# A graph layer on one core: 126 rows instead of 128 per gather, 51 fillers instead of 53, and the first list of single rows ahead of the block numbers

## The chip, the cores and the metric

One core of one Trainium2 chip runs the whole program. The metric is the device time of one execution in microseconds (us). The kernel before takes 15128.52 us, the median of three runs (15126.48 to 15129.18). One more execution was profiled: it took 15126.4 us, of which the span from its first to its last instruction is 15124.7 us.

## The reference

The input is a graph of N = 50,000 nodes with 128 fp32 features each, and E = 1,650,000 edges (`src`, `dst`, a type of 0 or 1), sorted by `dst`. Each node has one edge to itself (a loop), so 50,000 of the edges have `src == dst`. Cut to what matters:

```python
Xs = X[src]                                   # one row of 512 bytes per edge
msg = jnp.where((edge_types == 0)[:, None], Xs @ W_data.T + b_data, Xs @ W_control.T + b_control)
agg = jax.ops.segment_sum(msg, dst, num_segments=N)
y = jax.nn.relu(agg + X @ W_self.T + b_self)
out = _layernorm(X + y, axis=-1)
```

Since the message is linear in the row, the kernel first sums the rows of `x` per destination node and type, and multiplies by the weights once per node.

## The kernel before, in words

**Blocks and steps.** The sorted list of edges is cut into NBLK = 431 blocks. A block is worked on in Q = 2 steps, and a step of an ordinary block takes 1917 edges, whose rows of `x` reach SBUF in three ways:

- R = 14 gathers of 128 rows each (`SIZES = [P] * R`, 1792 edges). A gather is one indirect DMA on GpSimd (POOL) with a list of row numbers, line 551 in `gathers`.
- S = 72 single rows, each a DMA of 512 bytes with its address in a register: the list of step 0 is issued by SyncE (SP), that of step 1 by ScalarE (ACT), line 585 in `single_rows`. Ahead of each 24 of them the queue loads 24 addresses into registers (line 580).
- F = 53 fillers. An edge that is a loop needs no gathered row, as the row of `x` is there anyway. So each loop among the 1792 edges leaves a hole, and the kernel puts the edge of a filler in its place. `fill` (lines 388 to 417) does it on VectorE (DVE) with arrays of 30 x 63 numbers per partition (63 = F + LATE, LATE = 10 being the fillers that may be handed on to the next step); a loop's own row comes in by `left_out_columns` to `left_out_rows`.

Block 0 and the last block are plain: they have gathers alone. The last block takes what is left, 1640 edges in 13 gathers: twelve of 128 rows and one of 104.

**What a block does then.** DVE compares each edge's column with the numbers 0 to 127 (`onehot`, line 507: which of 64 nodes, which type) and counts per column (line 515). TensorE (PE) multiplies the gathered rows by the one-hot matrices (line 607; line 613 for the 72 single rows) into PSUM, DVE adds that to the block's sums (line 621), PE applies the weights (lines 641 to 651), DVE and ACT do the layer norm, and SP stores 124 nodes.

**What sets the order.** The instructions stand on each engine in the order in which the program writes them. What matters around the change:

- POOL does nothing but gathers after its first few microseconds. `y`, into which a step's 14 gathers go, has five buffers, so POOL may be up to five steps ahead of PE.
- `pace` (lines 533 to 542) holds POOL back against the lists of single rows: from block FAR = 4 on, the k-th gather of block b waits until SP and ACT have both issued the lists of all blocks up to b, and k of 28 parts of the lists of block b + 1. SP and ACT count that up as they issue.
- The lists are issued up to FAR = 4 blocks ahead, into ten buffers (five for each queue), which PE gives back after line 613.
- At the start, `columns(0)` computes the first ten blocks' columns and the byte addresses of the single rows (line 191) on DVE. `block_numbers` (lines 236 to 248) computes, also on DVE but some 25 us later, where each block's nodes begin, and `window(0)` lets SP load these numbers into registers (line 483) and fetch a stretch of the transposed `x` (line 490). Ahead of the loop over the blocks stand, in this order: `columns(0)`, `spread(1)`, `fill(1)`, `block_numbers()`, `window(0)`, work on the blocks 0 to 2, and the lists `single_rows(1)` to `single_rows(3)`.

If some step had more than LATE fillers waiting to be handed on, a flag would be set at the end, and a second, general version of the layer would run after this one (`general`). In the profile it doesn't run.

Of the kernel before, what the change touches and what calls it, by code (L numbers as in the profile page):

```python
# [26 lines left out]
P = 128  # L27
# [6 lines left out]
R = 14  # L34
# [2 lines left out]
PASS = 7  # L37
B = 124
C = R * Q
F = 53  # L40
LATE = 10
FX = LATE + F
R1 = R + 1
H = R + 1
C1 = Q * R1
SIZES = [P] * R
SIZE = sum(SIZES)
CE = Q * SIZE
S = 72
LOAD = 24  # L50
BE = CE + Q * (F + S)
NBLK = 2 + (E + LATE - CE) // BE
REST = E + LATE - CE - (NBLK - 2) * BE
REST_ROWS = [min(n, max(0, REST - q * SIZE - sum(SIZES[:r]))) for q in range(Q) for r, n in enumerate(SIZES)]
RCH = sum(n > 0 for n in REST_ROWS)
assert len(SIZES) == R and sum(REST_ROWS) == REST
GB = 10
# [4 lines left out]
FAR = 4  # L62
# [29 lines left out]
def plain(b):  # L92

    return b == 0 or b >= NBLK - 1
# [6 lines left out]
def straight(ctx, tc, c, x, x_t, edges_t, edges_f, edges_1, dst_first, first_p, out):  # L101
# [70 lines left out]
    fills_f = keep.tile([P, 1], F32, name="fills_f")  # L172
    nc.vector.memset(fills_f, float(F))
    last_f = keep.tile([P, 1], F32, name="last_f")
# [112 lines left out]
    def columns(g):  # L287
        for _ in column_steps(g):
            pass

    def column_steps(g):
# [82 lines left out]
        stay = eds.tile([P, GB, C1], F32, name="stay")  # L374
        nc.vector.scalar_tensor_tensor(stay, rk, F - LOOP, v, op0=ALU.is_ge, op1=ALU.mult)
        col_g[g], rk_g[g], stay_g[g], cb_g[g], vp_g[g] = col, rk, stay, cb, v_f
# [3 lines left out]
    def spread(b):  # L380

        if plain(b):
            return
        g, i = divmod(b, GB)
        vf = lists[b % 2][:, :Q * FX]
        nc.tensor.matmul(vf, row_of[:, i:i + 1].to_broadcast([STACK, P]), vp_g[g], start=True, stop=True)

    def fill(b):

        if plain(b):  # L390
            return
        g, i = divmod(b, GB)
        two = lists[b % 2]
        vf, cb = two[:, :Q * FX], two[:, Q * FX:]
        nc.vector.tensor_copy(cb, cb_g[g][:, i, :])  # L395
        m = fil.tile([P, C1, FX], F32, name="m", bufs=1)
        nc.vector.tensor_tensor(m, rk_g[g][:, i, :, None].to_broadcast([P, C1, FX]),  # L397
                                rank_no_ps[:, None, :].to_broadcast([P, C1, FX]), op=ALU.is_equal)
        new = fil.tile([P, C1, FX], F32, name="new", bufs=1)
        nc.vector.tensor_tensor(new.rearrange("p (q r) f -> p q r f", r=R1), m.rearrange("p (q r) f -> p q r f", r=R1),  # L400
                                vf.rearrange("p (q f) -> p q f", f=FX)[:, :, None, :].to_broadcast([P, Q, R1, FX]),
                                op=ALU.mult)
        v = fil.tile([P, C1], F32, name="v_new")
        nc.vector.tensor_reduce(v, new, AX.X, ALU.add)  # L404
        vi = fil.tile([P, C1], I32, name="vi")
        nc.vector.tensor_tensor(vi, v, stay_g[g][:, i, :], op=ALU.add)
        idx = fil.tile([P, C1], I32, name="idx", bufs=RAHEAD + 2)
        nc.vector.tensor_single_scalar(idx, vi, COLS.bit_length() - 1, op=ALU.logical_shift_right)
        nc.vector.scalar_tensor_tensor(col_g[g][:, i, :], idx, -float(COLS), vi, op0=ALU.mult, op1=ALU.add)
        idxs[b] = idx  # L410

        old = fil.tile([P, C1, FX], F32, name="new", bufs=1)
        nc.vector.tensor_tensor(old, m, cb[:, :, None].to_broadcast([P, C1, FX]), op=ALU.mult)  # L413
        by = fil.tile([P, Q, FX], BF16, name="by")
        with nc.allow_low_precision(reason="whole numbers below 256, one of them not 0"):
            nc.vector.tensor_reduce(by, old.rearrange("p (q r) f -> p q f r", r=R1), AX.X, ALU.add)  # L416
        bys[b] = by
# [37 lines left out]
    def column(k):  # L455
        return k // R * R1 + k % R
# [54 lines left out]
    def counts(b):  # L511

        cnt = ohp.tile([P, Q, 2 * W], BF16, name="cnt")
        with nc.allow_low_precision(reason="whole numbers up to R1"):
            nc.vector.tensor_reduce(cnt, ohs[b].rearrange("p (q r) w -> p q w r", r=R1), AX.X, ALU.add)  # L515
        cnts[b] = cnt
# [12 lines left out]
    def mark(q):  # L529
        (nc.scalar if q else nc.sync).sem_inc(issued[q], 1)  # L530
        issued_no[q] += 1

    def pace(b, k):

        if b < FAR:
            return
        for q in range(Q):
            if (b + LAG, q) in marks:
                n = marks[b + LAG, q] + k
                if n > asked[q]:  # L540
                    nc.gpsimd.wait_ge(issued[q], n)
                    asked[q] = n

    def gathers(b, ks):
# [3 lines left out]
        for k in ks:  # L548
            pace(b, k)
            r = REST_ROWS[k] if b == NBLK - 1 else SIZES[k % R]  # L550
            copy = nc.gpsimd.indirect_dma_start(  # L551
# [16 lines left out]
    def single_rows(b):  # L568
        if plain(b):
            return  # L570
        g, i = divmod(b, GB)
        for q in range(Q):
            j = alone_no[0] % ALONE
            alone_no[0] += 1
            marks[b, q] = issued_no[q]
            y = one.tile([S, D], F32, name="y1")
            for s0 in range(0, S, LOAD):
                n = min(LOAD, S - s0)
                at = i * Q + q
                _, regs = nc.values_load_multi_w_load_instructions(  # L580
                    off_g[g][at:at + 1, s0:s0 + n], engines=[ACT if q else SP], min_val=0, max_val=(N - 1) * ROW,
                    skip_runtime_bounds_check_because=CLAMPED)
                for k, r in enumerate(regs):
                    r = nc.s_assert_within(r, 0, (N - 1) * ROW, skip_runtime_bounds_check_because=CLAMPED)
                    copy = (nc.scalar if q else nc.sync).dma_start(y[s0 + k:s0 + k + 1, :].bitcast(U8),  # L585
                                               x_bytes[bass.ds(r, ROW)].rearrange("(p e) -> p e", e=ROW))
                    copy.then_inc(alone[j], 16)
                    tc.no_tile_sem_insts.add(copy.ins.name)
                    tc.add_to_no_dep_group(f"single{b}_{q}", copy.ins)
                    while issued_no[q] - marks[b, q] < (s0 + k + 1) * C // S:  # L590
                        mark(q)
            got[j] += 16 * S
            singles[b, q] = y, alone[j], got[j]

    def products(b, q, ks):
# [9 lines left out]
        for k in ks:  # L605
            r = REST_ROWS[k] if b == NBLK - 1 else SIZES[k % R]
            nc.tensor.matmul(acc[:, :2, :].rearrange("p t w -> p (t w)"), y[:r, k % R, :], ohs[b][:r, column(k), :],  # L607
# [116 lines left out]
        nc.vector.tensor_copy(c["bad"], total)  # L724

    columns(0)
    spread(1)
    fill(1)
    block_numbers()
# [9 lines left out]
    for b in range(1, AHEAD):  # L739
        onehot(b)  # L740
        counts(b)
    for b in range(1, FAR):
        single_rows(b)
    made, fresh = 2, [2]
    ready = []
# [72 lines left out]
    b = NBLK - 1  # L818
# [230 lines left out]
def gnn_resnorm(  # L1049
# [46 lines left out]
    with ExitStack() as own:  # L1096
        straight(own, tc, c, x, x_t, edges_t, edges_f, edges_1, dst_first, first_p, out)
# [61 lines left out]
```

## Time and profile before

| | |
|---|---|
| median of three runs | 15128.52 us |
| profiled execution | 15126.4 us |
| its span | 15124.7 us |
| first gather starts / last gather ends | 3.33 us / 15109.26 us |
| gathers | 12,053 |
| busy share of POOL, DVE, PE, PE's weight loads, ACT | 75%, 80%, 38%, 36%, 0% |
| mean busy share of the 16 DMA engines | 20.1% for the gathers, 3.1% for the rest |

The instructions that issue a DMA on SP and ACT aren't counted as busy time, so ACT's 0% says nothing of how full its queue is. A POOL record of a gather ends when the gather has been handed to the DMA engines, not when its rows have landed. DVE has the highest share of busy time, but a share is an average: what counts is which engine never waits.

### The profile page before, as it was taken

What the parts mean: (1) busy time and instruction counts of PE and PEld (TensorE: products, weight loads), DVE (VectorE), ACT (ScalarE), POOL (GpSimd) and SP (SyncE); (2) the same over time, 40 slices, a digit from 0 to 9 for tenths busy, and PEclk for the clock granted to TensorE, in tenths of its full rate; (3) what the DMA queues carried; (4) which work ended last, traced back from release to release, by engine and by line L of the source; (5) the groups of instructions that cost most, each with busy time, mean ns of one, the idle gap of its engine ahead of it and who ended that gap; (6) DMA issues with size and microseconds to landing.
All of it is one profiled execution on the core that took longest, in us unless ns stands there. A gap on an engine that the chain in (4) does not pass through costs nothing.

```text
span 15124.7 us, 261323 instructions
## 1 busy us (share of the span) xinstructions
PE 5807.3 (38%) x32944; PEld 5433.6 (36%) x32945; DVE 12113.2 (80%) x12021; ACT 67.2 (0%) x222; POOL 11400.6 (75%) x12063
## 2 busy tenths in 40 slices
PE   3434333333333333333333333333333333333333
PEld 3333333333333333333333333333333333333333
DVE  9888888878787787888887778787888888778785
ACT  0000000000000000000000000000000000000000
POOL 6777777777777777777777777777777777777777
PEclk7666666666666666666666666666666666666666
DMA  2222222222222222222222222222222222222222
GB/s 60 61 62 60 61 60 60 61 60 61 61 60 60 61 60 60 61 60 60 61 60 60 63 60 62 60 60 62 60 60 62 60 60 61 61 60 61 60 60 57
DMA packets 583259, 916.02 MB, mean 61 GB/s; under 512 B 259900, under 2 KB 375957, under 8 KB 581474
## 3 DMA queue, kind: packets, MB, share of 16 engines
q0 software_dynamic: 385696, 790.66, 20.1%
q1 hardware_dynamic: 133564, 92.41, 2.2%
q10 hardware_dynamic: 62214, 16.14, 0.5%
q14 instruction: 1518, 12.44, 0.3%
q8 instruction: 267, 4.37, 0.1%
HBM read 870.81 MB, written 27.36 MB: 59 GB/s over the span
## 4 chain that ended last, share of the span: by engine, by line
ACTq 29%; SPq 21%; PE 19%; issue 16%; DMA 10%; POOL 3%; DVE 2%; PEldq 0%; PEld 0%; POOLq 0%; ACT 0%; DVEq 0%
ACTq L585 24%; PE acc L607 18%; SPq L585 17%; DMA y<-in_x,idx 10%; ACTq L580 5%; SPq L580 3%; POOL y L551 3%; PE acc L613 1%; ACTq L530 1%; SPq L530 0%; PE rank L320 0%; DVE cnt L515 0%; DVE by L416 0%; PE acc L616 0%; PEldq L558 0%
## 5 line engine op out<-in xcount | busy, mean ns | idle before, releaser
L551 POOL DMA_INDIRECT y<-in_x,idx x12040 | 11386.8, 946 | 3703.5 <-issue 1808.4
L607 PE MATMUL acc<-oh,y 128*128 128x128 f32 x24106 | 4731.8, 381 | 9047.4 <-PEq L558 8980.3
L607 PEld LDWEIGHTS acc<-oh,y 128*128 128x128 f32 x24106 | 4529.5, 290 | 9357.9 <-issue 5094.8
L515 DVE TENSOR_REDUCE cnt<-oh 128x256 bf16<-128x3840 f32 x431 | 2840.3, 6590 | 14.7
L507 DVE TENSOR_TENSOR oh<-col,small 128x3840 f32<-128x3840 f32 x431 | 1786.1, 4144 | 0.0
L416 DVE TENSOR_REDUCE by<-new 128x126 bf16<-128x1890 f32 x429 | 1500.3, 3497 | 14.6
L621 DVE TENSOR_TENSOR sums<-acc,sums 128x192 f32 x861 | 307.8, 357 | 1333.9 <-PE acc L616 1283.9
L395 DVE COPY small<-cb 128x30 f32<-128x30 f32 x429 | 82.5, 192 | 1246.3 <-PE small L423 1243.3
L400 DVE TENSOR_TENSOR new<-m,small 128x1890 f32<-128x1890 f32 x429 | 911.3, 2124 | 14.7
L397 DVE TENSOR_TENSOR m<-rk,small 128x1890 f32<-128x1890 f32 x429 | 911.3, 2124 | 14.6
L404 DVE TENSOR_REDUCE v_new<-new 128x30 f32<-128x1890 f32 x429 | 910.4, 2122 | 14.7
L413 DVE TENSOR_TENSOR new<-m,small 128x1890 f32<-128x1890 f32 x429 | 907.9, 2116 | 0.0
L613 PE MATMUL acc<-oh,y 72*128 72x128 f32 x1716 | 333.7, 275 | 0.0
L651 PE MATMUL po<-wmsgT,sums 128*124 128x128 f32 x1724 | 304.1, 299 | 0.0
L613 PEld LDWEIGHTS acc<-oh,y 72*128 72x128 f32 x1716 | 265.4, 194 | 0.0
L641 PE MATMUL po<-own_w,xT 128*124 128x256 f32 x862 | 260.2, 383 | 0.8 <-DVE h L657 0.8
L637 DVE TENSOR_TENSOR sums<-pl,sums 128x372 f32<-128x372 f32 x429 | 233.9, 545 | 15.0
L651 PEld LDWEIGHTS po<-wmsgT,sums 128*124 128x124 f32 x1724 | 221.2, 187 | 52.8 <-issue 0.9
L448 DVE TENSOR_TENSOR pl<-pl,xT 128x248 f32<-128x248 f32 x429 | 182.2, 425 | 46.7 <-DVE xT L501 2.8
L649 PE MATMUL po<-bias,sums 3*124 3x128 f32 x862 | 207.1, 319 | 0.8 <-DVE sums L621 0.8
L649 PEld LDWEIGHTS po<-bias,sums 3*124 3x124 f32 x862 | 124.1, 181 | 146.8 <-issue 145.4
L431 DVE TENSOR_SCALAR z<-node_no,at 126x256 bf16<-126x256 f32 x429 | 162.9, 380 | 15.2
(148 smaller groups left out, 2871.8 us busy)
## 6 DMA issues: line engine op xcount, KB each, us to landing
y<-in_x ACTq DMA_DIRECT2D x30888, 0.5 KB
y<-in_x SPq DMA_DIRECT2D x30888, 0.5 KB
y<-in_x,idx POOLq DMA_INDIRECT x12040
xw<-in_x_t SPq DMA_DIRECT2D x54, 496.0 KB
out<-o SPq DMA_DIRECT2D x431, 62.0 KB
sdt<-in_edges_t SPq DMA_DIRECT2D x44, 450.0 KB
sdt_f<-in_edges_f SPq DMA_DIRECT2D x44, 14.8 KB
sd<-in_edges SPq DMA_DIRECT2D x44, 5.6 KB
```

Of the source, the lines that this page charges most:

```text
L397: nc.vector.tensor_tensor(m, rk_g[g][:, i, :, None].to_broadcast([P, C1, FX]), rank_no_ps[:, None, :].to_broadcast([P, C1, FX]), op=ALU.is ...
L400: nc.vector.tensor_tensor(new.rearrange("p (q r) f -> p q r f", r=R1), m.rearrange("p (q r) f -> p q r f", r=R1), vf.rearrange("p (q f) -> ...
L404: nc.vector.tensor_reduce(v, new, AX.X, ALU.add)
L413: nc.vector.tensor_tensor(old, m, cb[:, :, None].to_broadcast([P, C1, FX]), op=ALU.mult)
L416: nc.vector.tensor_reduce(by, old.rearrange("p (q r) f -> p q f r", r=R1), AX.X, ALU.add)
L507: nc.vector.tensor_tensor(oh, col_g[g][:, i, :, None].to_broadcast([P, C1, 2 * W]), num_ps[:, None, :].to_broadcast([P, C1, 2 * W]), op=AL ...
L515: nc.vector.tensor_reduce(cnt, ohs[b].rearrange("p (q r) w -> p q w r", r=R1), AX.X, ALU.add)
L551: copy = nc.gpsimd.indirect_dma_start(out=y[:r, k % R, :].bitcast(U8), out_offset=None, in_=x_rows, in_offset=bass.IndirectOffsetOnAxis(ap ...
L580: _, regs = nc.values_load_multi_w_load_instructions(off_g[g][at:at + 1, s0:s0 + n], engines=[ACT if q else SP], min_val=0, max_val=(N - 1 ...
L585: copy = (nc.scalar if q else nc.sync).dma_start(y[s0 + k:s0 + k + 1, :].bitcast(U8), x_bytes[bass.ds(r, ROW)].rearrange("(p e) -> p e", e ...
L607: nc.tensor.matmul(acc[:, :2, :].rearrange("p t w -> p (t w)"), y[:r, k % R, :], ohs[b][:r, column(k), :], start=k == of_step[0], stop=k = ...
L613: nc.tensor.matmul(acc[:, :2, :].rearrange("p t w -> p (t w)"), y, ohs[b][:S, q * R1 + R, :], start=False, stop=True)
```

## The change

Three constants and one line. A gather takes P - 2 = 126 rows, F is 51, and `single_rows(1)` is issued right after `columns(0)`; what depends on the constants (the number of blocks, the layout of the edge lists) follows by itself.

```diff
-F = 53
+F = 51
 LATE = 10
 FX = LATE + F
...
-SIZES = [P] * R
+SIZES = [P - 2] * R
 SIZE = sum(SIZES)
...
     columns(0)
+    single_rows(1)
     spread(1)
     fill(1)
     block_numbers()
...
-    for b in range(1, FAR):
+    for b in range(2, FAR):
         single_rows(b)
```

A step now takes 14 x 126 + 72 + 51 = 1887 edges instead of 1917, so there are 438 blocks instead of 431, and the last one takes 1018 edges: eight gathers of 126 rows and one of 10. A gather's rows are dealt to the transfer engines in equal parts: 128 rows are 16 times 8, 126 rows are 14 times 9.

On POOL, the order of the gathers stays and their number and size change. From the first gather to the end of the layer there stand, in the kernel before (`idx` and `sdt` hold the row numbers):

```order
L155 IOTA node_no 126x256
L551 DMA y<-in_x,idx_123 128x512 x28
L551 DMA y<-in_x,idx 128x512 x12012
L551 DMA y<-in_x,sdt 128x512 x12
L551 DMA y<-in_x,sdt 104x512
```

and in the changed kernel:

```order
L155 IOTA node_no 122x256
L551 DMA y<-in_x,idx_123 126x512 x28
L551 DMA y<-in_x,idx 126x512 x12208
L551 DMA y<-in_x,sdt 126x512 x8
L551 DMA y<-in_x,sdt 10x512
```

That is 12,245 gathers instead of 12,053, 192 more.

On SP, at the start, the queue holds after the first loads, in the kernel before (line 483 waits for the block numbers, line 580 for the addresses of the single rows; `y_376` is block 1's buffer, `y_872` block 2's):

```order
L220 DMA two_p<-in_first_p 10x176
L483 TENSOR_LOAD base_i
L490 DMA xw<-in_x_t 128x3968
L580 TENSOR_LOAD off
L585 DMA y_376<-in_x 1x512 x24
L580 TENSOR_LOAD off
L585 DMA y_376<-in_x 1x512 x24
L580 TENSOR_LOAD off
L585 DMA y_376<-in_x 1x512 x24
L580 TENSOR_LOAD off
L585 DMA y_872<-in_x 1x512 x24
```

and in the changed kernel (block 1's buffer is `y_277` here):

```order
L220 DMA two_p<-in_first_p 10x176
L580 TENSOR_LOAD off
L585 DMA y_277<-in_x 1x512 x24
L580 TENSOR_LOAD off
L585 DMA y_277<-in_x 1x512 x24
L580 TENSOR_LOAD off
L585 DMA y_277<-in_x 1x512 x24
L483 TENSOR_LOAD base_i
L490 DMA xw<-in_x_t 128x3968
L580 TENSOR_LOAD off
L585 DMA y_872<-in_x 1x512 x24
```

The 72 single rows of block 1 with their three loads stand ahead of the load of the block numbers, which used to stand ahead of them. ACT's order stays: its queue had no such load.

## The prediction

> **What bounds the kernel now.** First the page's busy shares, then POOL's group over the steady part of the run (400 to 15,000 us; after the bar its busy time, the mean ns of one gather, and POOL's idle time ahead of them), then two neighbours of the timeline, and POOL's list of waits over the whole run (total us, times, longest).
>
> ```profile
> PE 5807.3 (38%) x32944; PEld 5433.6 (36%) x32945; DVE 12113.2 (80%) x12021; ACT 67.2 (0%) x222; POOL 11400.6 (75%) x12063
> ```
>
> ```profile
> L551 POOL DMA_INDIRECT y<-in_x,idx x11673 | 11038.5, 946 | 3562.8 <-issue 1727.3 <-ACTq L530 946.1 <-SPq L530 855.4
> ```
>
> ```profile
> 7012.16 0.94 POOL L551 DMA_INDIRECT y<-in_x,idx  x1 [0.30 <-issue]
> 7013.40 0.94 POOL L551 DMA_INDIRECT y<-in_x,idx  x1 [0.30 <-ACTq L530]
> ```
>
> ```profile
> POOL y L551 <- issue: 1811.8, 5937, 0.3
> POOL y L551 <- ACTq L530: 985.9, 3146, 26.0
> POOL y L551 <- SPq L530: 872.2, 2850, 2.4
> ...
> POOL y L551 <- PE acc L607: 1.2, 2, 0.9
> ```
>
> DVE's 80% is the highest share, but POOL decides. Its 11,673 steady gathers fill 11038.5 + 3562.8 = 14601.3 of the 14,600 us, 1250.9 ns each. The idle part, 0.30 us ahead of each, is no wait, whatever name stands behind it: it is as long in every row. In the whole run just three waits are longer, 26.0, 2.4 and 0.9 us. So a block lasts 28 gathers, 35.0 us, and the run is the number of gathers times their period. The check: 12,053 x 1.2509 = 15077.1, plus 27.75 and 0.55 for the waits above 0.30, plus 3.3 ahead of the first gather and 15.4 behind the last, is 15124.1; the span is 15124.7.
>
> Next is who would come after POOL. DVE's largest idle time stands ahead of line 621, where it waits for PE, which waits for gathered rows; and the lists of single rows have some room (timeline; start, length, queue, count):
>
> ```profile
> L621 DVE TENSOR_TENSOR sums<-acc,sums 128x192 f32 x861 | 307.8, 357 | 1333.9 <-PE acc L616 1283.9 <-PE acc L613 30.2 <-PE acc L607 4.2
> ```
>
> ```profile
> 7026.47 29.22 SPq L585 DMA_DIRECT2D y<-in_x  x72
> 7055.91 0.28 SPq L691 DMA_DIRECT2D out<-o  x1
> 7063.06 29.49 SPq L585 DMA_DIRECT2D y<-in_x  x72
> ```
>
> ```profile
> 7009.09 65.52 ACTq L585 DMA_DIRECT2D y<-in_x  x144
> 7074.79 0.30 ACT L677 ACTIVATE sd<-mv,eps 124x2 f32<-124x2 f32 x1 [70.39 <-DVE at L430]
> 7080.14 59.89 ACTq L585 DMA_DIRECT2D y<-in_x  x132
> ```
>
> SP needs some 31 us per block. ACT needs 65.52 + 0.30 us for two blocks and a first load of addresses (under 2 us), 33.8 us per block of the 35.0 that POOL gives it. That is the floor if gathers got cheaper: 1207 ns per gather, 44 ns below today.
>
> **The change part by part.**
>
> *More gathers.* 12,245 instead of 12,053. 192 x 1.2509 = **+240.2 us**, with no cover, as POOL never waits. The seven blocks' other work lies beside POOL.
>
> *The first list.* At the start POOL has its one real wait (POOL's timeline, then SP's, then ACT's, then SP's wait for the block numbers):
>
> ```profile
> 143.77 0.95 POOL L551 DMA_INDIRECT y<-in_x,idx  x1 [0.31 <-issue]
> 170.71 0.94 POOL L551 DMA_INDIRECT y<-in_x,idx  x1 [25.98 <-ACTq L530]
> 174.02 0.99 POOL L551 DMA_INDIRECT y<-in_x,idx  x1 [2.37 <-SPq L530]
> ```
>
> ```profile
> 43.60 0.37 SPq L490 DMA_DIRECT2D xw<-in_x_t  x1
> 45.56 91.50 SPq L585 DMA_DIRECT2D y<-in_x  x216
> 137.25 0.37 SPq L196 DMA_DIRECT2D sdt<-in_edges_t  x1
> ...
> 140.32 154.69 SPq L585 DMA_DIRECT2D y<-in_x  x360
> ```
>
> ```profile
> 15.09 188.36 ACTq L585 DMA_DIRECT2D y<-in_x  x432
> ```
>
> ```profile
> SPq L483 <- DVE shift L246: 37.5, 1, 37.5
> ```
>
> The 26 us are put down to ACT, but ACT was done: its four lists (288 of 432 rows) ended at 15.09 + 288 x 0.436 = 140.7. SP had stood 37.5 us for the block numbers, began its fourth list at 140.32 and ended it 30.9 us later, at 171. That is when POOL went on. In the changed kernel SP begins at about 15.1, like ACT. A list takes 30.5 us (91.50 / 3), so list 1 ends at 45.6; the load and `xw` come to 47.6, and the first row of list 2 at 49.2; list 3 ends at 110, the edge loads at 113, list 4 at 144. Block 4's gathers can't start before 143.77 + 0.95 + 0.31 = 145.0. So both waits go: 25.68 + 2.07 = **-27.75 us**.
>
> What is late next? Three things could be, and all have room:
>
> ```profile
> 55.73 0.40 DVE L501 COPY xT<-xw 128x124 f32 x1 [0.46 <-issue]
> ```
>
> ```profile
> 120.24 3.34 PE L607 MATMUL acc<-oh,y 128*128 128x128 f32 x28
> ```
>
> ```profile
> 164.01 0.18 DVE L408 TENSOR_SCALAR idx<-vi 128x30 int32<-128x30 int32 x1
> ```
>
> `xw` is issued 4 us later than at 43.60, and DVE wants it at 55.73: at the worst DVE starts 4 us later. Block 4's first buffer is that of block 1's second step, which PE has finished by 124, 21 us ahead of 145. Block 5's row numbers are there at 164, and POOL wants them at 145.0 + 28 x 1.25 = 180. If that cover were gone, a part of the 27.75 us would stay.
>
> *Fewer fillers.* Five instructions of a fill run over 30 x 63 numbers, now 30 x 61:
>
> ```profile
> L416 DVE TENSOR_REDUCE by<-new 128x126 bf16<-128x1890 f32 x429 | 1500.3, 3497 | 14.6
> L400 DVE TENSOR_TENSOR new<-m,small 128x1890 f32<-128x1890 f32 x429 | 911.3, 2124 | 14.7
> L397 DVE TENSOR_TENSOR m<-rk,small 128x1890 f32<-128x1890 f32 x429 | 911.3, 2124 | 14.6
> L404 DVE TENSOR_REDUCE v_new<-new 128x30 f32<-128x1890 f32 x429 | 910.4, 2122 | 14.7
> L413 DVE TENSOR_TENSOR new<-m,small 128x1890 f32<-128x1890 f32 x429 | 907.9, 2116 | 0.0
> ```
>
> (3497 + 2124 + 2124 + 2122 + 2116) x 2/63 = 380 ns per block on DVE, which waits for PE anyway: **0**. Counted from the inputs, a step's 1764 gathered edges hold 53.5 loops on average for 51 fillers, and at most 2 are handed on, where 10 may be; so the general version doesn't run.
>
> *The gather itself.* Its price decides. The sum so far is 15126.4 + 240.2 - 27.75 = 15338.9 us if a gather of 126 rows costs what one of 128 costs, and **each ns moves it by 12.245 us**. Break-even is at -17.3 ns. The trace shows no gather of 126 rows over 14 engines. It shows one of another shape: the run's last, 104 rows, 13 engines with 8 rows each (line 551 by its row numbers, ns as minimum/median/maximum; the last two of the timeline; the queue of the gathers):
>
> ```profile
> L551 POOL DMA_INDIRECT y<-in_x,idx x12040: 940/944/1605, 3.3 to 15091.5; - x198
> ...
> L551 POOL DMA_INDIRECT y<-in_x,sdt x13: 940/944/987, 15092.7 to 15108.3; - x13
> ```
>
> ```profile
> 15107.02 0.95 POOL L551 DMA_INDIRECT y<-in_x,sdt  x1 [0.30 <-issue]
> 15108.27 0.99 POOL L551 DMA_INDIRECT y<-in_x,sdt  x1 [0.30 <-issue]
> ```
>
> ```profile
> q0 software_dynamic: 385696, 790.66, 20.1%
> ```
>
> With 24 rows and three engines fewer it took 987 ns, 43 more than the median of 944. No DVE instruction ran beside it (a window over it: its length, then busy time of PE, PEld, DVE, ACT, POOL):
>
> ```profile
> 15108.00:15109.20 1.20, 0.10 (x1) 0.00 (x0) 0.00 (x0) 0.00 (x0) 0.93 (x1) 1.00 0.36 105
> ```
>
> And 385,696 packets are 32 for each of the 12,053 gathers, the last one included: an engine without rows still gets its packets, so leaving engines out saves none of them. Both rows speak for a price above that of 128 rows: 43 ns for a shape that doesn't use all 16 engines. On top, 14 engines take nine rows each where 8 were taken. One row more for every engine costs nothing if the 944 ns are fixed, and 944/8 = 118 ns if nothing in them is. No row divides them. I take a third, 40 ns: nearer to the lower end, as 24 rows fewer saved nothing that shows. So a gather costs 43 + 40 = +83 ns, between +43 and +161: 12.245 x 83 = **+1016 us**, with ends of +527 and +1971.
>
> The Trainium skill, page "DMA: Bandwidth & Descriptors", section "Anatomy of one DMA — SWDGE (gpsimd) path", calls descriptor generation "small, variable" and says that many descriptors can be emitted before their cost shows; by that rule the ninth row is free, and the sum is 15,865 us. No row here tests it.
>
> The sum: 15338.9 + 1016 = 16,355 us. It is made against the profiled execution, 2.1 us below the median of the runs shown.
>
> **The rivals.**
>
> *Engines carry the price (faster).* If POOL spends its time per engine served, 944/16 = 59 ns each, two fewer save 118 ns, and any saving over 17.3 ns wins. Beyond 44 ns ACT's lists hold POOL through `pace`: 437 blocks x 33.8 us and some 60 us at the ends are 14,830 us. For it: no row shows what the 944 ns consist of. Against it: 13 engines took 43 ns more, and idle engines get packets. The time is 14,830 to 15,096 us; chance 0.17.
>
> *Rows carry the price (about the same).* 944 x 2/128 = 15 ns saved: 15,158 us, 0.2% above. Against it: 104 rows should have taken 767 ns. Chance 0.05.
>
> *No price at all.* The 987 ns belong to the last gather of the run and not to its shape, and both shapes cost 944: 15,339 us. For it: it is a single sample. Chance 0.12.
>
> *The first list brings nothing*, as DVE's work at the start holds POOL instead: 27.75 us more in every case, which decides no sign.
>
> **How the numbers follow.** The forecast, a price of 43 ns or more, has 0.66; its own range is 15,865 to 17,310 us, its middle 16,355. Slower by over 0.2% (what a measurement of this kernel can tell from no change) is that and the case without a price, 0.78; within 0.2% is 0.05, faster 0.17. The range goes from 15,120, which takes in the case of the same time and leaves the faster one out, to 17,000 us, a price of 136 ns; above it I leave 0.03.
>
> **What would show it.** The median of line 551 in the changed kernel: 987 ns is the lower end, about 1027 the forecast, 944 or less a rival. Steady POOL without a wait, period 1.33 us; DVE's idle time ahead of line 621 grown by 2 to 3 us per block; no wait of POOL above 0.3 us near 145 us; SP's first single row near 15 us. The forecast is wrong if line 551 is below 927 ns, or if POOL waits for ACT in every block.

## The result, and the profile after

The changed kernel takes 15960.98 us (median of four runs, 15959.55 to 15962.81), the kernel before 15128.85 us in the same measurement: a ratio of 1.0551, 95% interval 1.0538 to 1.0564. The profiled execution took 15962.81 us with a span of 15961.0 us.

First the page's busy shares of the changed kernel, then POOL's group over 400 to 15,000 us, and POOL's list of waits over the whole run (total us, times, longest).

```profile
PE 5923.7 (37%) x33461; PEld 5544.7 (35%) x33462; DVE 12203.4 (76%) x12186; ACT 68.4 (0%) x226; POOL 12210.3 (77%) x12255
```

```profile
L551 POOL DMA_INDIRECT y<-in_x,idx x11214 | 11181.0, 997 | 3419.4 <-issue 1646.3 <-ACTq L530 920.8 <-SPq L530 834.6
```

```profile
POOL y L551 <- issue: 1834.4, 6016, 0.3
POOL y L551 <- ACTq L530: 987.0, 3237, 0.3
POOL y L551 <- SPq L530: 892.2, 2926, 0.3
```

In this stretch POOL still never waits: (11181.0 + 3419.4) / 11,214 = 1302.0 ns per gather, 51.1 more than before. The idle time ahead of a gather has stayed at 0.3 us, so all of it lies in the gather's own record, whose mean went from 946 to 997. The three long waits are gone: behind the first gather none is above 0.3 us any more.

Line 551 by its row numbers (ns as minimum/median/maximum), and the gathers' DMA queue:

```profile
L551 POOL DMA_INDIRECT y<-in_x,idx x12236: 990/996/1592, 3.2 to 15932.9; - x198
...
L551 POOL DMA_INDIRECT y<-in_x,sdt x9: 887/996/998, 15934.2 to 15944.6; - x9
```

```profile
q0 software_dynamic: 587744, 791.56, 19.3%
```

The median is 996 ns, 52 above 944. The least, 887, is the run's last gather, 10 rows on 10 engines. The queue has 587,744 packets: 48 for each of the 12,244 gathers of 126 rows, where there were 32, and 32 for the last gather. 48 are three per engine, on the two engines without rows as well. Nine rows of 512 bytes no longer fit the one packet of 4096 bytes that held eight.

The start: SP's queue (the view ends at 130 us, within the fourth list), and POOL where block 4's gathers begin (the one at 149.91 us, 112 gathers behind the first).

```profile
15.93 29.47 SPq L585 DMA_DIRECT2D y<-in_x  x72
46.59 0.36 SPq L490 DMA_DIRECT2D xw<-in_x_t  x1
48.54 60.54 SPq L585 DMA_DIRECT2D y<-in_x  x144
109.26 0.37 SPq L196 DMA_DIRECT2D sdt<-in_edges_t  x1
...
112.37 17.48 SPq L585 DMA_DIRECT2D y<-in_x  x44
```

```profile
148.60 1.00 POOL L551 DMA_INDIRECT y<-in_x,idx  x1 [0.30 <-issue]
149.91 1.00 POOL L551 DMA_INDIRECT y<-in_x,idx  x1 [0.31 <-issue]
151.21 1.00 POOL L551 DMA_INDIRECT y<-in_x,idx  x1 [0.30 <-SPq L530]
```

SP begins at 15.93 instead of 45.56, its fourth list at 112.37 instead of 140.32, and POOL walks into block 4 at 149.91 without a stop. On DVE, the waits for PE have grown and the fills have become shorter:

```profile
L621 DVE TENSOR_TENSOR sums<-acc,sums 128x192 f32 x875 | 312.8, 358 | 1733.5 <-PE acc L616 1692.6 <-PE acc L613 17.5 <-PE acc L607 7.9
L395 DVE COPY small<-cb 128x30 f32<-128x30 f32 x436 | 83.6, 192 | 1587.4 <-PE small L423 1587.4
L397 DVE TENSOR_TENSOR m<-rk,small 128x1830 f32<-128x1830 f32 x436 | 898.4, 2061 | 14.9
L416 DVE TENSOR_REDUCE by<-new 128x122 bf16<-128x1830 f32 x436 | 1536.2, 3523 | 15.0
```

Line 397 lost 63 ns, nearly the 67 that 2/63 of its 2124 ns are; line 416 lost nothing (3523 against 3497 ns). The sum of the result, in the prediction's terms: 15338.9 + 12.245 x 51.1 = 15964.6, and 15962.81 was measured.

### The profile page after: what moved, and what is told of

It reads as the page before. It is cut to its first block, busy times and chain, and to the rows that moved or that the text cites. A ratio compares the mean times of both kernels' runs of the same rounds, so it can differ in the third digit from the quotient of the medians.

```text
span 15961.0 us, 265504 instructions
## 1 busy us (share of the span) xinstructions
PE 5923.7 (37%) x33461; PEld 5544.7 (35%) x33462; DVE 12203.4 (76%) x12186; ACT 68.4 (0%) x226; POOL 12210.3 (77%) x12255
## 3 DMA queue, kind: packets, MB, share of 16 engines
q0 software_dynamic: 587744, 791.56, 19.3%
## 4 chain that ended last, share of the span: by engine, by line
ACTq 30%; SPq 20%; PE 19%; issue 16%; DMA 10%; POOL 3%; DVE 2%; PEldq 0%; PEld 0%; POOLq 0%; ACT 0%; DVEq 0%
ACTq L585 25%; PE acc L607 18%; SPq L585 17%; DMA y<-in_x,idx 10%; ACTq L580 5%; POOL y L551 3%; SPq L580 3%; PE acc L613 1%; ACTq L530 1%; DVE cnt L515 0%; SPq L530 0%; DVE by L416 0%; DVE oh L507 0%; PE rank L320 0%; PE acc L616 0%
## 5 line engine op out<-in xcount | busy, mean ns | idle before, releaser
L551 POOL DMA_INDIRECT y<-in_x,idx x12236 | 12200.0, 997 | 3731.8 <-issue 1832.3
L607 PE MATMUL acc<-oh,y 126*128 126x128 f32 x24490 | 4830.9, 383 | 9759.9 <-PEq L558 9739.1
L607 PEld LDWEIGHTS acc<-oh,y 126*128 126x128 f32 x24490 | 4624.8, 292 | 10074.4 <-issue 5483.0
L515 DVE TENSOR_REDUCE cnt<-oh 128x256 bf16<-128x3840 f32 x438 | 2883.8, 6584 | 14.9
L416 DVE TENSOR_REDUCE by<-new 128x122 bf16<-128x1830 f32 x436 | 1536.2, 3523 | 15.0
L400 DVE TENSOR_TENSOR new<-m,small 128x1830 f32<-128x1830 f32 x436 | 898.5, 2061 | 15.2
L397 DVE TENSOR_TENSOR m<-rk,small 128x1830 f32<-128x1830 f32 x436 | 898.4, 2061 | 14.9
L404 DVE TENSOR_REDUCE v_new<-new 128x30 f32<-128x1830 f32 x436 | 897.5, 2058 | 15.2
L413 DVE TENSOR_TENSOR new<-m,small 128x1830 f32<-128x1830 f32 x436 | 895.5, 2054 | 0.0
L501 DVE COPY xT<-xw 128x124 f32 x438 | 119.7, 273 | 74.2 <-issue 66.6
```

What stands on the lines that cost most here:

```text
L551: copy = nc.gpsimd.indirect_dma_start(out=y[:r, k % R, :].bitcast(U8), out_offset=None, in_=x_rows, in_offset=bass.IndirectOffsetOnAxis(ap ...
```

## The experiments

Twelve runs in three sets. The first set takes the change apart; the second and third measure the price of a gather's shape. The times of the second set can't be set beside the others: on its chip the kernel before itself took 19523.39 us. The profiles of the four kernels there show that SP and ACT needed longer for their single rows and that POOL waited for them; the kernel before wasn't profiled there. The kernels with 120 and 112 rows ran again in the third set, where their gathers took as long (within 1 ns), so the durations of the second set are used and its times are not.

**The first list alone** (`e1_order_only`): the kernel before with this edit.

```diff
     columns(0)
+    single_rows(1)
     spread(1)
...
-    for b in range(1, FAR):
+    for b in range(2, FAR):
```

> The kernel before with nothing changed but the place of block 1's single rows. My theory: SP starts its lists near 16 us, POOL's waits of 25.68 and 2.07 us ahead of block 4 go, the period of a gather stays 1.251 us: 15126.4 - 27.75 = 15,099 us, 0.18% faster. Rival: DVE's work at the start holds POOL instead (through the five gather buffers or the row numbers), a wait of about as long comes a little later, and the time stays at 15,129 us.

Measured: 15101.99 us against 15128.39, ratio 0.9983, interval 0.9974 to 0.9992; the medians differ by 26.4 us. POOL's longest waits are now

```profile
POOL y L551 <- issue: 1811.7, 5938, 0.3
POOL y L551 <- ACTq L530: 955.3, 3128, 0.9
POOL y L551 <- SPq L530: 873.0, 2860, 0.3
```

so the rival is out: nothing took the wait's place but 0.55 us at ACT (the wait of 0.9 us less the usual 0.30). This version beats both kernels.

**The shape and the fillers alone** (`e2_shape_only`): 126 rows and 51 fillers, with the list where it was.

```diff
-F = 53
+F = 51
-SIZES = [P] * R
+SIZES = [P - 2] * R
```

> 126 rows and 51 fillers, but the single rows of block 1 where they were. My theory: POOL reaches block 4 at 3.2 + 112 x 1.302 = 149 us and stands until SP ends its fourth list at 171 us, then about 2 us more for the first part of list 5: 15,961 + 23 = 15,984 us. The move is then worth less beside slow gathers than beside fast ones (23 against 28 us). Rival: gathers that are 52 ns longer would have taken the wait away without the move, as POOL comes later: 15,961 us.

Measured: 15983.8 us (15981.65 to 15986.84), ratio 1.0565, interval 1.0551 to 1.058; 22.8 us above the changed kernel. POOL's timeline at block 4:

```profile
149.59 1.00 POOL L551 DMA_INDIRECT y<-in_x,idx  x1 [0.30 <-issue]
170.68 0.99 POOL L551 DMA_INDIRECT y<-in_x,idx  x1 [20.10 <-ACTq L530]
172.91 1.07 POOL L551 DMA_INDIRECT y<-in_x,idx  x1 [1.23 <-SPq L530]
```

The wait ends at 170.7 us as before and begins 6 us later, as the gathers are slower. The rival, that slower gathers take the wait away by themselves (15,961 us), is out. So the move is worth 26.4 us beside gathers of 128 rows and 22.8 beside gathers of 126.

**53 fillers with 126 rows** (`e4_53_fillers`): the changed kernel with

```diff
-F = 51
+F = 53
```

> The changed kernel with 53 fillers instead of 51: 437 blocks, 12,233 gathers instead of 12,245, and DVE's fills 63 numbers wide instead of 61. My theory: fills lie beside POOL's gathers, so only the number of gathers counts: 12 x 1.302 = 16 us less, 15,945 us. Rival: the fills are on the path: 437 x 0.38 = 166 us more, about 16,110 us.

Measured: 15945.11 us (15942.62 to 15948.42), ratio 1.054, interval 1.0525 to 1.0554; 15.9 us below the changed kernel, twelve gathers' worth. The fills are off the path, and two fillers more are worth a little.

**Fourteen gathers of many shapes** (`e3_mixed`): the kernel of the first experiment with

```diff
-F = 53
+F = 43
-SIZES = [P] * R
+SIZES = [128, 120, 104, 126, 128, 98, 112, 64, 128, 121, 119, 125, 10, 128]
```

> The 14 gathers of a step take 128, 120, 104, 126, 128, 98, 112, 64, 128, 121, 119, 125, 10 and 128 rows (43 fillers, 508 blocks, block 1's list moved); the duration of each of the 14 on POOL is what counts, not the time of the whole. Rows are dealt evenly to the largest number of engines up to 16 that divides them: 128 = 16x8, 120 = 15x8, 104 = 13x8, 126 = 14x9, 98 = 14x7, 112 = 16x7, 64 = 16x4, 121 = 11x11, 119 = 7x17, 125 = 5x25, 10 = 10x1. Theory A, a fixed price of some 43 ns for any shape with fewer than 16 engines and some 10 ns per row of an engine: 120 and 104 take 987 ns, 126 996, 98 975, 112 934, 64 900, 121 1015, 119 1075, 125 1160, 10 890. Theory B, each idle engine costs 14 ns and rows cost little: 120 takes 958, 104 987, 98 973, 121 1016, 119 1073, 125 1101, 112 and 64 944. Theory C, the 52 ns are the ninth row, which no longer fits the first packet of 4096 bytes, and the 987 ns of the last gather were its place in the run: 120, 104, 98, 112 and 64 take 944 or less, 126 996, and 121, 119, 125 each more.

Measured: 18345.61 us, and one step's gathers on POOL's timeline, in the order of the list:

```profile
9014.28 0.95 POOL L551 DMA_INDIRECT y<-in_x,idx  x1 [0.30 <-issue]
9015.54 0.98 POOL L551 DMA_INDIRECT y<-in_x,idx  x1 [0.30 <-SPq L530]
9016.83 0.98 POOL L551 DMA_INDIRECT y<-in_x,idx  x1 [0.30 <-ACTq L530]
9018.12 0.97 POOL L551 DMA_INDIRECT y<-in_x,idx  x1 [0.30 <-issue]
9019.39 0.98 POOL L551 DMA_INDIRECT y<-in_x,idx  x1 [0.30 <-ACTq L530]
9020.68 0.94 POOL L551 DMA_INDIRECT y<-in_x,idx  x1 [0.30 <-ACTq L530]
9021.93 0.95 POOL L551 DMA_INDIRECT y<-in_x,idx  x1 [0.30 <-issue]
9023.19 0.91 POOL L551 DMA_INDIRECT y<-in_x,idx  x1 [0.30 <-issue]
9024.40 0.96 POOL L551 DMA_INDIRECT y<-in_x,idx  x1 [0.30 <-issue]
9025.66 1.00 POOL L551 DMA_INDIRECT y<-in_x,idx  x1 [0.30 <-issue]
9026.97 1.10 POOL L551 DMA_INDIRECT y<-in_x,idx  x1 [0.30 <-ACTq L530]
9028.37 1.18 POOL L551 DMA_INDIRECT y<-in_x,idx  x1 [0.30 <-SPq L530]
9029.85 0.88 POOL L551 DMA_INDIRECT y<-in_x,idx  x1 [0.30 <-ACTq L530]
9031.03 0.96 POOL L551 DMA_INDIRECT y<-in_x,idx  x1 [0.30 <-ACTq L530]
```

The outcome is mixed. Rows per engine cost: 0.88 us with one (10 rows), 1.00 with 11, 1.10 with 17, 1.18 with 25. But 126 rows take 0.97 here and not 0.996, and 128 rows take 0.95 to 0.98 and not 0.944, by what stands ahead of them. None of the three theories has room for that, so this run can't tell the price of a shape; a shape has to be measured among its like.

**Two shapes among their like, and two pairs** (second set). The edits, each in the kernel of the first experiment:

```diff
-F = 53
+F = 48
-SIZES = [P] * R
+SIZES = [120] * R
```

> Every gather takes 120 rows, 15 engines with 8 rows each (48 fillers, 459 blocks, 12,837 gathers, block 1's list moved): against 128 rows one engine is left out and the rows per engine stay. Theory A, the shape sets the price and any shape with fewer than 16 engines costs some 43 ns: median 987 ns, period 1.295 us, 16,645 us. Theory B, 14 ns per idle engine: 958 ns, 16,270 us. Theory H, what costs is a change of shape from one gather to the next, and a row of gathers of one shape with 8 rows per engine takes 944 ns whatever the engines: 16,090 us; the 52 ns of 126 rows would then be the ninth row's.

```diff
-F = 53
+F = 46
-SIZES = [P] * R
+SIZES = [112] * R
```

> Every gather takes 112 rows, 16 engines with 7 rows each (46 fillers, 490 blocks, 13,704 gathers, block 1's list moved): all engines, one row less for each. If a row of an engine costs some 12 ns: median 932 ns, period 1.240 us, 17,015 us. If it costs nothing in a run of one shape: 944 ns, 17,180 us. If the price goes by rows: 826 ns; POOL would then wait for ACT's lists.

```diff
-F = 53
+F = 52
-SIZES = [P] * R
+SIZES = [128, 126] * 7
```

> Gathers of 128 and of 126 rows take turns (52 fillers, 434 blocks, block 1's list moved). If each shape has its price whatever its neighbours: 944 and 996 ns in turn, 970 on average. If a change of shape costs by itself: the 128 behind a 126 takes about 983 ns as in the run of mixed shapes, and the 126 behind a 128 is not 996; the average is then not 970, and by the mixed run's 983 it is above it.

```diff
-SIZES = [P] * R
+SIZES = [128] * 13 + [126]
```

> One gather in 14 takes 126 rows, the other 13 take 128 (53 fillers, 431 blocks, block 1's list moved). If each shape has its price: thirteen gathers at 944 ns, one at 996. If the shape before counts: the 126 behind 128s takes about 987 to 996, the first 128 behind it about 983, the next ones between that and 944; how many are raised says how long one odd gather is felt.

Measured, in this order: 21026.94, 21983.37, 19723.79 and 19401.13 us, and line 551 of the first two:

```profile
L551 POOL DMA_INDIRECT y<-in_x,idx x12824: 978/982/1907, 3.3 to 20980.2; - x198
```

```profile
L551 POOL DMA_INDIRECT y<-in_x,idx x13692: 927/933/1542, 3.2 to 21931.8; - x199
```

120 rows take 982 ns: leaving out one engine costs 38 ns with the same eight rows per engine. Theory A holds, with 38 ns in place of 43; B (958) and H (944) are out. 112 rows on all 16 engines take 933 ns: a row of an engine costs 11 ns, and the price doesn't go by rows (826).

Alternating gathers, and the one 126 among 128s with its neighbours:

```profile
9014.58 0.97 POOL L551 DMA_INDIRECT y<-in_x,idx  x1 [0.30 <-issue]
9015.85 0.98 POOL L551 DMA_INDIRECT y<-in_x,idx  x1 [0.30 <-issue]
9017.14 0.97 POOL L551 DMA_INDIRECT y<-in_x,idx  x1 [0.31 <-issue]
```

```profile
7043.99 0.94 POOL L551 DMA_INDIRECT y<-in_x,idx  x1 [0.30 <-issue]
7045.24 0.98 POOL L551 DMA_INDIRECT y<-in_x,idx  x1 [0.30 <-issue]
7046.52 0.97 POOL L551 DMA_INDIRECT y<-in_x,idx  x1 [0.30 <-issue]
```

Over the run, the medians of the alternating kernel are 983 ns for 128 rows and 971 for 126, 977 on average where the two uniform kernels give 970. So a price that a shape has whatever its neighbours is out, and the average lies above 970, as expected where a change of shape costs by itself. The single 126 takes 980 (987 to 996 were expected), the 128 behind it 972 (983 were expected), and the next ones 942 to 944 again. So an odd shape is felt in its own record and in the next one: together the single 126 costs 36 + 28 = 64 ns, 12 more than the 52 of a 126 among 126s, and an alternating pair takes 1954 ns, 14 more than 944 + 996. If a record merely booked part of a gather's work to its successor, both sums would stay; what the 12 to 14 ns are is not shown.

**The sum, and the time beside it** (third set): 98 rows are 14 x 7, 104 rows 13 x 8; the kernels with 120 and 112 rows are the same as above, on a chip where POOL decides.

```diff
-F = 53
+F = 39
-SIZES = [P] * R
+SIZES = [98] * R
```

> Every gather takes 98 rows, 14 engines with 7 rows each (39 fillers, 557 blocks, 15,580 gathers, block 1's list moved): as many engines as 126 rows have, two rows per engine fewer. If the price is a sum of some 38 ns for leaving engines out and some 12 ns per row of an engine, as 944, 982 and 932 ns for 128, 120 and 112 rows say: 970 ns; and where POOL decides, 15,580 x 1.278 + 18 = 19,930 us. If the engines left out cost nothing by themselves beside rows that fill less than a packet: 932 ns, 19,340 us.

```diff
-F = 53
+F = 42
-SIZES = [P] * R
+SIZES = [104] * R
```

> Every gather takes 104 rows, 13 engines with 8 rows each (42 fillers, 526 blocks, 14,717 gathers, block 1's list moved): the shape of the last gather in the kernel before, as a rule instead of once. If the price doesn't go by the number of engines left out: 982 ns as with 15 engines, 19,010 us where POOL decides. If each engine left out costs: three times what one costs, 944 + 3 x 38 = 1058 ns, 20,130 us. If the last gather's 987 ns came from its place: 944 ns, 18,450 us.

> The kernel with 120 rows in every gather once more, for its time beside a kernel before that POOL bounds. Median 982 ns as in its first run, period 1.290 us: 12,837 x 1.290 + 18 = 16,580 us, if the gathers' price decides; more only if the lists of single rows hold POOL again.

> The kernel with 112 rows in every gather once more, for its time beside a kernel before that POOL bounds. Median 932 to 933 ns, period 1.240 us: 13,704 x 1.240 + 18 = 17,010 us. A block then has 34.7 us for ACT's two lists of 67.6 us per two blocks (33.8 us each), so that ACT is nearly, but not yet, the bound.

Line 551 of the four, in this order:

```profile
L551 POOL DMA_INDIRECT y<-in_x,idx x15568: 965/969/2072, 3.3 to 19866.6; - x200
...
L551 POOL DMA_INDIRECT y<-in_x,sdt x12: 965/966/1247, 19867.9 to 19881.9; - x12
```

```profile
L551 POOL DMA_INDIRECT y<-in_x,idx x14700: 978/982/1603, 3.3 to 18953.6; - x199
...
L551 POOL DMA_INDIRECT y<-in_x,sdt x17: 982/982/1347, 18954.9 to 18975.8; - x17
```

```profile
L551 POOL DMA_INDIRECT y<-in_x,idx x12824: 977/983/1690, 3.3 to 16538.4; - x198
```

```profile
L551 POOL DMA_INDIRECT y<-in_x,idx x13692: 928/933/1568, 3.2 to 17005.7; - x199
...
L551 POOL DMA_INDIRECT y<-in_x,sdt x12: 929/934/1565, 17006.9 to 17020.5; - x12
```

The times are 19900.95, 18993.56, 16571.1 and 17040.48 us, beside 15129.22 for the kernel before: within 0.2% of what period times number gave each (19,930, 19,010, 16,580 and 17,010). All shapes together, as medians among their like:

| rows | engines x rows each | ns |
|---|---|---|
| 112 | 16 x 7 | 933 |
| 128 | 16 x 8 | 944 |
| 98 | 14 x 7 | 969 |
| 104 | 13 x 8 | 982 |
| 120 | 15 x 8 | 982 to 983 |
| 126 | 14 x 9 | 996 |

Thirteen engines cost what fifteen cost, so the 38 ns are paid once and not per engine left out. A row of an engine costs 11 ns (112 to 128) or 13.5 (98 to 126, two rows, 27 ns). It goes on like that far out: the last gathers of three kernels have 58, 74 and 106 rows on two engines, 29, 37 and 53 each, and take 1247, 1347 and 1565 ns (the maxima above), 12.5 to 13.6 ns per row. At the other end, the changed kernel's last gather, with one row per engine, takes 887 ns, 95 less than the 982 of eight rows, 13.6 ns per row. These four gathers stand behind another shape, so their slopes are rough.

The number of packets doesn't set the price. The kernels with 98, 104 and 120 rows have 32 packets per gather (498,608, 471,008 and 410,784 in all), as many as gathers of 128 rows. From eight to nine rows a gather has 16 packets more and takes 14 ns longer; from seven to eight (969 to 982) it has none more and takes 13 ns longer.

What isn't settled: every shape with fewer than 16 engines also has a number of rows that is no multiple of 16. Which of the two costs the 38 ns no run tells, since no such gather leaves the two apart.

## Why the prediction was right, and where its sizes were off

- *POOL bounds the kernel, and the time is gathers times period.* Right, in all runs but those where single rows were slow to issue.
- *192 more gathers, +240.2 us.* Right: the time follows from the number of gathers and the period in the changed kernel and in the third set.
- *The first list, -27.75 us.* Right: 26.4 us measured alone, 22.8 beside slower gathers. The wait that the trace put down to ACT was SP's, as worked out from the two queues: moving SP's list alone removed it. The three covers named for what comes next held.
- *Fewer fillers, 0.* Right on the path: going back to 53 changed the time by the number of gathers. On DVE the saving was smaller than worked out, as line 416 didn't get shorter.
- *The gather's price, +83 ns between +43 and +161.* The mechanism, one price for a shape that leaves engines out and another for the ninth row, was right, and a size was off. The 43 ns read from the run's last gather were 38 in a run of such gathers, 5 too many. The ninth row, put at 40 ns because "I take a third", costs 14 (982 to 996), 26 less. That step failed: 118 ns, its upper end, took all of the 944 ns to be rows. The slope of 11 to 13.5 ns per row says that eight rows are some 100 ns of them, a tenth rather than a third. So the price was 51 to 52 ns instead of 83, and 31.9 x 12.245 = 391 us of the 394 between forecast and median are explained by it.
- *A last gather read as a price list.* One sample of 987 ns among 12,053 carried the forecast. The same row stands in the kernel with the first list moved alone, 987 again, and a kernel of such gathers gives 982. That the sample was off by 5 ns only was luck: it stood behind gathers of 128 rows, and a single 126 in such a place took 980 ns where its like take 996.
- *The Trainium skill*, page "DMA: Bandwidth & Descriptors", section "Anatomy of one DMA — SWDGE (gpsimd) path", was quoted for descriptors whose cost hardly shows. The runs agree with "small": 11 to 13.5 ns per row of an engine. Small isn't nothing where 12,245 gathers stand in a row: the nine against eight rows are 14 x 12.245 = 171 us. By the section "Rules for kernel authors" of the same page of the Trainium skill a transfer should use all 16 engines; here it is POOL's own 38 ns that speak for it.
- *The rivals.* Engines that carry the price: out, fifteen cost more than sixteen. Rows that carry the price: out, 112 rows took 933 ns and not 826. No price: out.
- *The signs.* The median of line 551 came out at 996 ns, above the lower end of 987 and below the forecast 1027, and the period at 1.302 us instead of 1.33. SP's first single row stood at 15.93 us, and no wait was left near 145 us. DVE's idle time ahead of line 621 grew from 3.1 to 4.0 us per block, less than the 2 to 3 us forecast, and ahead of line 395 from 2.9 (1246.3 us over 429 blocks) to 3.6: a block has become 28 x 51 = 1.4 us longer and DVE's work 0.2 us shorter, and DVE waits for that at both places.

## What to carry to other kernels

Where one engine issues back to back, count its instructions and their period first: one ns on each of 12,245 gathers is 12 us, so a shape is measured among its like, as a whole kernel of it, ahead of any saving that it promises elsewhere. Rows of an odd shape (a remainder at the end of a run) are a free sample of a price, good for the sign and a bound. A wait for two queues is put down to one of them; which it was is read from the times at which each was done.

## What the runs showed of the hardware

- A gather costs POOL 11 to 14 ns per row of an engine, however many engines share it, and 38 ns once if it doesn't spread over 16 engines with a multiple of 16 rows. Engines without rows get packets all the same: 16 x 2 per gather with 128 rows, 16 x 3 with 126.
- The time on POOL's record depends on the gather ahead: 128 rows take 944 ns behind 128, 972 behind a single 126 and 983 where the two alternate.
- The kernel with 120 rows ran on two chips. In the second set SP took 43.22 us to issue 72 single rows, where the same kernel took 29.24 us in the third, and POOL waited for the lists in nearly every block (SP's timeline and POOL's waits, second set); the gathers' own 982 ns were the same. Whether the chip or the occasion made the difference is open, as each ran once.

```profile
7013.98 43.22 SPq L585 DMA_DIRECT2D y<-in_x  x72
```

```profile
POOL y L551 <- SPq L530: 3785.9, 2461, 5.3
POOL y L551 <- issue: 2969.6, 9007, 3.0
POOL y L551 <- ACTq L530: 1251.6, 1011, 50.8
```
